# Four column groups for the ranking sums of layer 0's experts, and the masks' verdict ahead of them

## The chip, the cores and the metric

The kernel runs on one core of a Trainium2 chip. The metric is the device time of one execution in microseconds (us). Four engines compute: TensorE (PE, with its weight load listed apart as PEld), VectorE (DVE), ScalarE (ACT) and GpSimd (POOL). SyncE (SP) issues most of the transfers. Each engine works through its own list of instructions in order, and they wait for one another by semaphores.

## What is computed

The network has four layers, each a cross-attention of 2048 tokens (256 values each) with 1601 context rows, followed by a feed-forward block. The change concerns the first feed-forward block, a mixture of eight experts:

- The tokens are normed, multiplied with a gate matrix (256 x 8), and the eight scores of every token go through eight rounds of Sinkhorn normalization: columns are scaled to sum one, then rows.
- Every expert takes the 256 tokens (2048/8) with its highest scores. For that, every token needs its rank within each expert: how many tokens have a higher score, with ties settled by position.
- A token taken by several experts keeps the output of one. The expert's output is the normed token times that expert's 256 x 256 matrix; it is multiplied with the score and added to the token.

Two inputs are attention masks, int32, 2048 x 1601 each. The kernel looks at both of them at the start. If they have a certain form (all rows alike and only the last 400 columns ever open), the layers that use them can work on 400 context rows.

## The kernel before, in words

**Order of the program.** `network` runs `attention0` (layer 0's attention, which drives the look at the masks as a generator beside its own work), then `experts0`, then `verdict`. `verdict` (L286 on) multiplies the flags `some` with ones on PE (L293), casts the result to an integer on DVE (L294), and every engine loads it into a register (L295). A conditional follows: its first branch holds the layers with masked tails (`attention1_tail` first), the other one the general layers. What stands inside the conditional isn't mixed with what stands ahead of it. Outside of the regions named below, a scheduler at compile time settles the order on each engine; it may bring a transfer forward as soon as its buffer is free. `experts0` issues its two loads of expert weights `w_e` (L514, 1 MB each, SP) and that of the gate matrix `gw` (L531) at its head.

**Buffers.** The weights go into a ring of three buffers that lives through the whole program. Other buffers belong to pools that a stage opens and closes. A later stage's pool may lie where an earlier one's was.

**experts0.** 16 token tiles of 128, four chunks of 512. From the head of the stage on (after the constants), PE, ACT, DVE and POOL are kept in program order (`manual_schedule`), so the order written is the order run:

- Norm and gating for each chunk: statistics (L139, L140), inverse root on POOL (L145), scaling (L151), transposes (L173), copies `xe` (L177), then the gate product (L605).
- A generator `ahead` makes the products of one token tile with all eight experts, in four pieces. One piece is two matmuls of 512 columns in float32 (L568, four records in the profile, in `products`), a copy out of PSUM on ACT (L578), and after every second piece a write to a table in DRAM (L581). `step(ahead, 1)` makes one piece. Steps are placed in the norm, in the Sinkhorn rounds and in the ranking.
- Sinkhorn, eight rounds (L620 to L631).
- The ranking goes over eight experts `e` and 16 tiles `t`. `row` (L643, L647) spreads one expert's scores of a chunk over all partitions. For a tile `t`, DVE compares that row `bc` with the tile's own scores (L683, and L688 for the seven tiles below `short`), which gives `ge`, 128 x up to 2048 ones and zeros. `count` sums `ge` over the partitions on PE (L656), with the 128 x 8 matrix `pick` as weights, which puts the sum into row `e` of a PSUM tile `rk`. For tiles below `short` ACT also sums `ge` along its rows (L662). `count` for a tile is placed after the next tile's comparisons (`late`). There are three `ge` buffers.
- Then `rk` is copied to `rT` (L701), transposed to tokens (L707), and a chain of small DVE instructions settles which expert each token takes (L703 to L730).
- For the 13 tiles below `early`, POOL gathers the taken expert's row from the table (L735, indirect DMA, four row buffers) and DVE adds it to the token (L755, `add_row`). The products of the last three tiles are made here on PE, two pieces at a time, and DVE adds each expert's part, weighted (L747).

**After it.** `attention1_tail` loads three weights (L203), transposes them on PE (L211), copies them (L220), and projects keys (L951) and values (L960). Its loop over chunks begins with a norm (L173) and the query projection (L974). `ffn1`'s weights `w_fc` and `w_pr` take the ring buffers of `w_e`.

Of the kernel before, what the change touches and what calls it, by code (L numbers as in the profile page):

```python
# [15 lines left out]
P = 128  # L16
# [38 lines left out]
class Net:  # L55
# [451 lines left out]
    def experts0(self):  # L507
# [11 lines left out]
        early = 13  # L519

        short = 7
        with ExitStack() as s:
# [3 lines left out]
            cp = s.enter_context(tc.tile_pool(name="e0c", bufs=3))  # L526
            stage = s.enter_context(tc.tile_pool(name="e0s", bufs=3))
            rows = s.enter_context(tc.tile_pool(name="e0r", bufs=4))
# [21 lines left out]
            for e in range(E):  # L550
                nc.vector.memset(pick[:, e, e : e + 1], 1.0)
            number = pool.tile([P, E], F32, name="number")
# [3 lines left out]
            table = [dram.tile([P * E, D], F32, name=f"table{t}") for t in range(early)]  # L556
# [16 lines left out]
            def ahead():  # L573
                todo = None

                def out():
                    t, h, y, ps = todo
                    nc.scalar.copy(y[:, h * 512 : (h + 1) * 512], ps)  # L578
                    if h % 2:
                        at = slice((h - 1) * 512, (h + 1) * 512)  # L580
                        nc.sync.dma_start(table[t].rearrange("(p e) d -> p (e d)", e=E)[:, at], y[:, at])  # L581

                for t in range(early):
                    y = stage.tile([P, NTOK], F32, name="y0")
# [50 lines left out]

            rk = [self.psc() for _ in range(2)]
            opened = set()
# [11 lines left out]
            def count(e, t, ge):  # L649

                cuts = [max(t * P, j * CH) for j in range(t // TPC, NCH)] + [NTOK]
                if e == 0 and (t + 1) * P not in cuts:
                    cuts.insert(1, (t + 1) * P)
                for lo, hi in zip(cuts, cuts[1:]):
                    j = lo // CH
                    nc.tensor.matmul(  # L656
                        rk[j // 2][0:E, j % 2, lo - j * CH : hi - j * CH], lhsT=pick[:, e, :], rhs=ge[:, lo:hi],
                        start=j not in opened, stop=e == E - 1 and t == 0,
                    )
                    opened.add(j)  # L660
                if t < short:
                    nc.scalar.activation(  # L662
                        seen[:, (t + 1) * P :], ge[:, (t + 1) * P :], AF.Copy, accum_out=far[:, t, e : e + 1]
                    )
# [4 lines left out]
            late = None  # L669
            for e in range(E):  # L670
                nxt = bcp.tile([P, NTOK], F32, name="bc") if e + 1 < E else None

# [5 lines left out]
                for n, t in enumerate(turns):  # L678
# [8 lines left out]
                    if to < NTOK:  # L687
                        nc.vector.tensor_scalar(ge[:, to:], bc[:, to:], own, None, ALU.is_le)  # L688
                    if late is not None:
                        count(*late)  # L690
                    late = (e, t, ge)
                    if nxt is not None and n in (6, 8, 10, 12):
                        row(e + 1, nxt, NCH - 1 - (n - 6) // 2)
                    if n in (1, 4, 7, 10, 13):
                        step(ahead, 1)
                bc = nxt
            count(*late)
            drain(ahead)
            rT = bcp.tile([P, NTOK], F32, name="bc")
            for j, copy in ((1, nc.vector.tensor_copy), (0, nc.scalar.copy)):  # L700
                copy(rT[0:E, j * 1024 : (j + 1) * 1024].rearrange("p (a b) -> p a b", a=2), rk[j][0:E])  # L701
# [4 lines left out]
            for t in range(NT):  # L706
                nc.tensor.transpose(ps[:, t * E : (t + 1) * E], rT[0:E, t * P : (t + 1) * P], self.ident[:E, :E])  # L707
# [25 lines left out]
            for t in range(early):  # L733
# [1108 lines left out]
def network(ctx: ExitStack, tc: tile.TileContext, a, out):  # L1842
# [5 lines left out]
    net.experts0()  # L1848
    n_odd = net.verdict()
    with tc.If(n_odd == 0) as masked:  # L1850
        net.attention1_tail("L1_xattn", masks[0])
        net.ffn1()
        net.attention1("L2_xattn", bias=True)
        net.ffn2()
        net.attention3_tail(masks[1])
        net.ffn3()
    with masked.Else():
        net.attention1("L1_xattn", mask=masks[0])
        net.ffn1()
        net.attention1("L2_xattn", bias=True)  # L1860
        net.ffn2()
        net.attention3()
        net.ffn3()
# [35 lines left out]
```

## Time and profile before

The profiled execution took 2056.5 us, of which 2054.8 are its span, first to last instruction. Three timed runs gave 2055.5, 2059.0 and 2063.3.

| What | us |
|---|---|
| median of the runs | 2059.0 |
| profiled execution | 2056.5 |
| its span | 2054.8 |
| PE busy | 1853.0 |
| DVE busy | 1085.2 |
| ACT busy | 827.1 |
| POOL busy | 642.4 |
| attention0's last add ends at | 710.1 |
| ranking's first comparison starts at | 755.8 |
| its last comparison ends at | 915.1 |
| last `add_row` ends at | 946.4 |
| `attention1_tail`'s first projection starts at | 954.4 |

Positions in the table and below are in us from the start of the span. A row of a chain or a timeline begins with the start and the duration in us; then come engine, line, operation, the tiles written and read and their shapes; `[1.30 <-PE x]` says how long the engine had been idle and what ended that. A chain of waits follows the work that ended last back from the end, so its rows are what set the time. A row of a table by stretches gives the stretch, its length, busy us and number of instructions of PE, PEld, DVE, ACT and POOL, then PE's granted clock, the transfer engines' busy share and GB/s. One float32 matmul shows as two records.

### The profile page before, as it was taken

The numbers are of one execution on the slowest core, as the hardware profiler recorded it, in microseconds if no ns is written. First come the engines' busy times: TensorE is split into PE (matmuls) and PEld (weight loads), VectorE is DVE, ScalarE is ACT, GpSimd is POOL, SyncE is SP. The second block draws the span as 40 slices with busy tenths as digits, with TensorE's granted clock in tenths as the row PEclk, the third lists the DMA queues.
The fourth block names the chain that finished last, engine by engine and source line by source line (L and its number), as shares of the span: only waits on it lengthen the run. The fifth ranks groups of instructions, "written<-read, shape, count | busy, mean of one in ns | idle before, by whom it ended". The sixth has DMA issues, their size and how long they took to land.

```text
span 2054.8 us, 22310 instructions
## 1 busy us (share of the span) xinstructions
PE 1853.0 (90%) x8533; PEld 919.9 (45%) x8533; DVE 1085.2 (53%) x2117; ACT 827.1 (40%) x1133; POOL 642.4 (31%) x418
## 2 busy tenths in 40 slices
PE   7889999999999899998977899999788788888899
PEld 3223333333333343333535764565567323233587
DVE  4666465555654358776455543232376477866300
ACT  4654434434434237761114331111153265654432
POOL 1168878868768500003001110000033101111100
PEclk9799999999999999999988999999988899999999
DMA  8830000000000021113000000000000000000461
GB/s 282 291 104 1 1 1 1 1 1 1 1 1 1 0 83 62 66 58 105 1 24 19 1 24 0 1 0 1 0 1 0 6 1 1 1 1 1 139 201 53
DMA packets 44066, 78.83 MB, mean 38 GB/s; under 512 B 5757, under 2 KB 32782, under 8 KB 43950
## 3 DMA queue, kind: packets, MB, share of 16 engines
q1 hardware_dynamic: 41520, 73.97, 10.6%
q0 software_dynamic: 624, 1.70, 0.3%
q10 hardware_dynamic: 1806, 1.64, 0.3%
q8 instruction: 69, 1.13, 0.2%
q14 instruction: 47, 0.39, 0.1%
HBM read 61.57 MB, written 15.73 MB: 38 GB/s over the span
## 4 chain that ended last, share of the span: by engine, by line
PE 71%; DVE 14%; ACT 6%; issue 3%; DMA 3%; POOL 2%; SPq 0%; ACTq 0%; DVEq 0%; POOLq 0%
PE pa L468 7%; PE psc L456 5%; PE psc L884 5%; PE pa L904 4%; PE pa L568 4%; PE psc L1682 3%; DVE mp L381 3%; PE psc L1820 3%; PE pa L1831 3%; PE psc L656 3%; DVE ri L418 3%; ACT p L1689 2%; PE psc L454 2%; PE pm L1732 2%; PE pm L376 2%
## 5 line engine op out<-in xcount | busy, mean ns | idle before, releaser
L477 POOL TENSOR_TENSOR sp<-sp,p 128x1024 f32<-128x1024 f32 (+1 forms) x176 | 418.5, 2378 | 58.0 <-ACT p L461 47.3
L381 DVE TENSOR_REDUCE mp<-pm 128x1 f32<-128x512 f32 x384 | 242.8, 680 | 160.7 <-PE pm L376 160.0
L461 ACT ACTIVATE p<-psc 128x1024 f32<-128x1024 f32 (+1 forms) x208 | 212.7, 1023 | 260.4 <-PE psc L456 162.3
L456 PE MATMUL psc<-qT,kT 64*128 64x512 f32 (+1 forms) x832 | 219.9, 591 | 0.0
L468 PE MATMUL pa<-p,v 128*64 128x512 f32 (+1 forms) x832 | 202.8, 609 | 0.0
L1689 ACT ACTIVATE p<-psc 100x1024 f32<-100x1024 f32 x128 | 124.0, 1021 | 77.1 <-PE psc L1682 69.6
L1668 DVE TENSOR_REDUCE ms<-psc 128x2 bf16<-128x800 f32 x128 | 123.0, 981 | 43.0 <-PE psc L1664 40.8
L376 PE MATMUL pm<-kb,qb 64*128 64x512 bf16 x384 | 100.5, 391 | 28.2 <-DVE mp L381 26.6
L144 POOL TENSOR_SCALAR rstd<-mv 128x4 f32<-128x4 f32 x32 | 8.7, 272 | 360.4 <-DVE mv L140 336.8
L468 PEld LDWEIGHTS pa<-p,v 128*64 128x64 f32 (+1 forms) x832 | 50.9, 137 | 132.7 <-issue 129.7
L568 PE MATMUL pa<-w_e,xe 128*128 128x512 f32 x208 | 103.0, 620 | 0.0
L884 PE MATMUL psc<-q,kT 128*128 128x512 f32 (+1 forms) x208 | 102.2, 610 | 0.0
L683 DVE SCALAR_TENSOR_TENSOR ge<-bc,g,after 128x128 bf16<-128x128 f32 (+8 forms) x128 | 79.0, 649 | 30.8 <-PE psc L656 23.6
L897 ACT ACTIVATE p<-psc 128x1024 f32<-128x1024 f32 (+1 forms) x28 | 26.9, 962 | 168.2 <-PE psc L893 168.2
L456 PEld LDWEIGHTS psc<-qT,kT 64*128 64x128 f32 (+1 forms) x832 | 85.6, 186 | 19.8 <-issue 6.6
L904 PE MATMUL pa<-v,p 128*128 128x257 f32 (+1 forms) x416 | 93.9, 381 | 0.0
L1724 POOL TENSOR_TENSOR attn<-o,ri 128x512 f32<-128x512 f32 x16 | 20.3, 1271 | 230.9 <-DVE ri L1722 209.6
L662 ACT ACTIVATE seen<-ge 128x1152 bf16<-128x1152 bf16 (+6 forms) x56 | 83.4, 1489 | 19.1 <-DVE ge L688 18.8
L454 PE MATMUL psc<-sh,negz 64*128 64x512 bf16 (+1 forms) x416 | 87.2, 384 | 2.1 <-ACT sh L403 2.0
L857 DVE TENSOR_REDUCE mp<-pm 128x1 f32<-128x512 f32 x64 | 34.4, 571 | 99.8 <-PE pm L852 99.7
L151 DVE TENSOR_SCALAR xn<-x,mv,rstd 128x256 f32<-128x256 f32 x128 | 51.6, 459 | 67.0 <-PE pm L173 65.8
L1682 PE MATMUL psc<-q,kT 32*100 32x512 f32 x512 | 75.6, 640 | 10.4 <-ACT p L1689 10.0
(359 smaller groups left out, 3228.7 us busy)
## 6 DMA issues: line engine op xcount, KB each, us to landing
w<-in_L_ffn_w_dram SPq DMA_DIRECT2D x16, 1024.0 KB, 6.3
table<-y SPq DMA_DIRECT2D x26, 512.0 KB, 2.6
head<-in_mask_BxSxS_ik_dram SPq DMA_DIRECT2D x16, 600.5 KB, 4.0
head<-in_mask_1x1xSxS_ik_dram SPq DMA_DIRECT2D x16, 600.5 KB, 4.1
tail<-in_mask_BxSxS_ik_dram SPq DMA_DIRECT2D x16, 200.0 KB, 4.1
tail<-in_mask_1x1xSxS_ik_dram SPq DMA_DIRECT2D x16, 200.0 KB, 3.9
x<-in_x_dram SPq DMA_DIRECT2D x16, 128.0 KB, 3.6
w_e<-in_L_ffn_experts_dram SPq DMA_DIRECT2D x2, 1024.0 KB, 7.2
```

The source lines that it names most:

```text
L376: nc.tensor.matmul(pair[j][:, :wd], lhsT=qb[h, i * P : (i + 1) * P], rhs=kb[h, hp, k0 : k0 + wd], start=True, stop=True,)
L381: nc.vector.tensor_reduce(mp[:, i, j, n : n + 1], pair[j][:, :wd], AX.X, ALU.max)
L454: nc.tensor.matmul(sc[:r, j, :], lhsT=negz[h, :r], rhs=sh[h, :], start=True, stop=False)
L456: nc.tensor.matmul(sc[:r, j, :], lhsT=kT[h, hp, kt * P : kt * P + r], rhs=q[h, :], start=False, stop=True,)
L461: nc.scalar.activation(p[:r], sc[:r], AF.Exp, scale=DH**-0.5)
L468: nc.tensor.matmul(acc[h, :], lhsT=v[:r, kt, hp * P + h.start : hp * P + h.stop], rhs=p[:r, j, :], start=kt == 0, stop=kt == NKT - 1,)
L477: nc.gpsimd.tensor_tensor(sums[:r], sums[:r], p[:r], ALU.add)
L568: nc.tensor.matmul(ps, lhsT=xnT[t // TPC][:, kc, (t % TPC) * P : (t % TPC + 1) * P], rhs=ew[kc][:, 2 * h : 2 * h + 2, :], start=kc == 0, s ...
L884: nc.tensor.matmul(sc[:r, j, :], lhsT=kT[:, kc, ks], rhs=q[:, kc, :], start=kc == 0, stop=False)
L904: nc.tensor.matmul(acc[:, : D + 1], lhsT=p[:r, kt, i * P : (i + 1) * P], rhs=v[:r, kt, :], start=kt == 0, stop=kt == NKT - 1,)
L1682: nc.tensor.matmul(sc[j // 2][:TR, j % 2, :], lhsT=kT[h, g, kt * TR : (kt + 1) * TR], rhs=q[u][h, :], start=True, stop=True,)
L1689: nc.scalar.activation(p[:TR], sc[k][:TR], AF.Exp, scale=DH**-0.5)
```

## The change

- The sums of four tiles are now issued together: `count` takes four tiles, and puts the sums of the k-th of them into partitions 32k to 32k+7 of `rk`, for one 512-column piece after the other. `rk` is set to zero first, by matmuls with a tile of zeros, and closed in the same way. The copies out of `rk` take all 128 partitions, and the transposes L707 become products with `fold`, a 128 x 8 matrix that adds the four groups.
- ACT's sum along rows is placed one tile later, in `along`. There are nine `ge` buffers for three.
- `early` is gone: all 16 tiles' products go through the table, 50 pieces of them in the ranking instead of 38, and 16 rows are gathered, with six row buffers for four. The products and weighted adds beside the gathers are gone.
- `verdict` runs ahead of `experts0`, which now stands in both branches of the conditional.

```diff
-            cp = s.enter_context(tc.tile_pool(name="e0c", bufs=3))
+            cp = s.enter_context(tc.tile_pool(name="e0c", bufs=9))
...
-            rows = s.enter_context(tc.tile_pool(name="e0r", bufs=4))
+            rows = s.enter_context(tc.tile_pool(name="e0r", bufs=6))
...
+            fold = pool.tile([P, E], F32, name="fold")
+            nc.vector.tensor_reduce(
+                fold, self.ident.rearrange("p (k r) -> p r k", k=4)[:, :E, :], AX.X, ALU.add
+            )
+            none = pool.tile([P, CH], BF16, name="none")
+            nc.gpsimd.memset(none, 0.0)
...
-                for t in range(early):
+                for t in range(NT):
                     y = stage.tile([P, NTOK], F32, name="y0")
...
+            def zeros(start, stop):
+                for j in range(NCH):
+                    nc.tensor.matmul(rk[j // 2][:, j % 2, :], lhsT=none[:, :P], rhs=none, start=start, stop=stop)
+
+            zeros(True, False)
...
-            def count(e, t, ge):
-
-                cuts = [max(t * P, j * CH) for j in range(t // TPC, NCH)] + [NTOK]
-                if e == 0 and (t + 1) * P not in cuts:
-                    cuts.insert(1, (t + 1) * P)
-                for lo, hi in zip(cuts, cuts[1:]):
-                    j = lo // CH
-                    nc.tensor.matmul(
-                        rk[j // 2][0:E, j % 2, lo - j * CH : hi - j * CH], lhsT=pick[:, e, :], rhs=ge[:, lo:hi],
-                        start=j not in opened, stop=e == E - 1 and t == 0,
-                    )
-                    opened.add(j)
-                if t < short:
-                    nc.scalar.activation(
-                        seen[:, (t + 1) * P :], ge[:, (t + 1) * P :], AF.Copy, accum_out=far[:, t, e : e + 1]
-                    )
+            def count(e, four):
+
+                for j in range(NCH):
+                    for k, (t, ge) in enumerate(four):
+                        lo = max(t * P, j * CH)
+                        if lo < (j + 1) * CH:
+                            nc.tensor.matmul(
+                                rk[j // 2][32 * k : 32 * k + E, j % 2, lo - j * CH :], lhsT=pick[:, e, :],
+                                rhs=ge[:, lo : (j + 1) * CH], start=False, stop=False,
+                            )
+
+            def along(e, t, ge):
+
+                nc.scalar.activation(
+                    seen[:, (t + 1) * P :], ge[:, (t + 1) * P :], AF.Copy, accum_out=far[:, t, e : e + 1]
+                )
...
+                    if long is not None:
+                        along(*long)
+                    long = (e, t, ge) if t < short else None
                     if late is not None:
                         count(*late)
-                    late = (e, t, ge)
+                        late = None
+                    four.append((t, ge))
+                    if len(four) == 4:
+                        late, four = (e, four), []
                     if nxt is not None and n in (6, 8, 10, 12):
                         row(e + 1, nxt, NCH - 1 - (n - 6) // 2)
-                    if n in (1, 4, 7, 10, 13):
+                    if n in (1, 3, 7, 9, 11, 15) or n == 13 and e < 2:
                         step(ahead, 1)
                 bc = nxt
+            along(*long) if long is not None else None
             count(*late)
             drain(ahead)
+            zeros(False, True)
             rT = bcp.tile([P, NTOK], F32, name="bc")
             for j, copy in ((1, nc.vector.tensor_copy), (0, nc.scalar.copy)):
-                copy(rT[0:E, j * 1024 : (j + 1) * 1024].rearrange("p (a b) -> p a b", a=2), rk[j][0:E])
+                copy(rT[:, j * 1024 : (j + 1) * 1024].rearrange("p (a b) -> p a b", a=2), rk[j])
...
             for t in range(NT):
-                nc.tensor.transpose(ps[:, t * E : (t + 1) * E], rT[0:E, t * P : (t + 1) * P], self.ident[:E, :E])
+                nc.tensor.matmul(
+                    ps[:, t * E : (t + 1) * E], lhsT=rT[:, t * P : (t + 1) * P], rhs=fold, start=True, stop=True
+                )
...
-            for t in range(early):
+            for t in range(NT):
                 row = rows.tile([P, D], F32, name="row")
...
-                if t % 2 == 0 and early + t // 4 < NT:
-                    tt, k = early + t // 4, t // 2 % 2
-                    sc = self.psc()
-                    for j in range(2):
-                        products(tt, 2 * k + j, sc[:, j, :])
-                    for e in range(4):
-                        nc.vector.scalar_tensor_tensor(
-                            self.x[tt], sc[:, e // 2, (e % 2) * D : (e % 2 + 1) * D],
-                            g[:, tt, 4 * k + e : 4 * k + e + 1], self.x[tt], ALU.mult, ALU.add,
-                        )
-            for t in range(early - 2, early):
+            for t in range(NT - 2, NT):
                 self.add_row(t, fetched[t], gate)
...
-    net.experts0()
     n_odd = net.verdict()
     with tc.If(n_odd == 0) as masked:
+        net.experts0()
         net.attention1_tail("L1_xattn", masks[0])
...
     with masked.Else():
+        net.experts0()
         net.attention1("L1_xattn", mask=masks[0])
```

More of the change, by code (lines that the diff above doesn't have):

```diff
@@ L516, in experts0 @@
             )
-        early = 13
         short = 7
@@ L555, in experts0 @@
             xnT = [pool.tile([P, 2, CH], F32, name=f"xe{c}") for c in range(NCH)]
-            table = [dram.tile([P * E, D], F32, name=f"table{t}") for t in range(early)]
+            table = [dram.tile([P * E, D], F32, name=f"table{t}") for t in range(NT)]
             g = pool.tile([P, NT, E], F32, name="g")
@@ L636, in experts0 @@
             rk = [self.psc() for _ in range(2)]
-            opened = set()
+            def zeros(start, stop):
+                for j in range(NCH):
+                    nc.tensor.matmul(rk[j // 2][:, j % 2, :], lhsT=none[:, :P], rhs=none, start=start, stop=stop)
+            zeros(True, False)
             def row(e, bc, c):
@@ L668, in experts0 @@
                 row(0, bc, c)
-            late = None
+            late = long = None
+            four = []
             for e in range(E):
```

## The prediction, on record before the changed kernel ran

> **What bounds the kernel now.** The page says PE is busy 90% of the span, so I read layer 0's experts (the change's place) and what touches it in four views.
>
> First the chain of waits, ranking loop (start, us, what):
>
> ```profile
> 815.78 2.16 PE psc L656 x10
> 818.14 0.59 PE psc L656 x2
> 818.73 1.91 PE pa L568 x4
> 820.65 1.18 PE psc L656 x7
> 821.82 1.91 PE pa L568 x4
> 823.74 0.80 PE psc L656 x4
> 824.53 0.58 PE pm L643 x4
> 825.37 1.91 PE pa L568 x4
> ...
> 835.96 2.16 PE psc L656 x10
> ```
>
> One expert takes 20.2 us (815.78 to 835.96), all of it PE: the sums (L656) 7.8, five products (L568) 9.4, rows (L643) and gaps 3.0. Second, busy times by stretch (PE, PEld, DVE, ACT, POOL), of this loop and of what follows it:
>
> ```profile
> 835.00:855.00 20.00, 19.79 (x77) 7.70 (x76) 16.05 (x40) 15.08 (x24) 0.00 (x0) 1.00 0.13 53
> 917.00:945.00 28.00, 24.77 (x66) 11.72 (x66) 19.47 (x50) 0.95 (x2) 12.78 (x13) 0.88 0.20 58
> ```
>
> Relieve PE and DVE is next at 16.05, then ACT at 15.1. Third, the timeline of the gather, a chain of POOL gathers beside the 48 product records:
>
> ```profile
> 918.01 1.87 PE L707 MATMUL pm<-ident,bc 8*128 8x8 f32 x16 [1.86 <-ACT bc L701]
> 919.81 22.87 PE L568 MATMUL psc<-w_e,xe 128*128 128x512 f32 x48
> 923.60 1.22 POOL L735 DMA_INDIRECT row<-table,index  x1 [200.74 <-DVE gate L730]
> 926.38 0.95 POOL L735 DMA_INDIRECT row<-table,index  x1 [0.30 <-issue]
> 946.36 0.14 DVE L294 CAST n_odd<-pm 1x1 int32<-1x1 f32 x1
> 947.22 0.38 SPq L203 DMA_DIRECT2D w_L_xattn<-in_L_xattn_Wk_dram  x1
> 954.38 4.72 PE L951 MATMUL pm<-ctxT,WkT 128*128 128x400 f32 x8
> ```
>
> Nothing after the branch is issued before the verdict: weights at 947.22, attention's first projection at 954.38. Fourth, the opening, where the chain of waits runs through the mask loads from 50 to 127 us; `w_e`, which today needs no verdict, is loaded inside that stretch:
>
> ```profile
> 68.39 0.39 SPq L514 DMA_DIRECT2D w_e<-in_L_ffn_experts_dram  x1
> ```
> ```profile
> 70.12 6.47 DMA head<-in_mask_1x1xSxS_ik_dram
> 76.68 1.30 ACT head L276 x2
> 78.00 3.79 DMA head<-in_mask_1x1xSxS_ik_dram
> ```
>
> **What the Trainium skill says.** "TensorEngine Tiling (Array Packing)", Tiling Modes: with outputs of at most 32 columns the array holds four 128x32 tiles that run in parallel. The trace agrees: L1699 (four heads, 100*32) ran 8 records in 1.07 us, where 8 full-width records take 8 x 0.43 = 3.4. "TensorE: Matmul & The Clock Gate", Part 1: after idling PE runs at half clock until some 3.4 us of work are done; here the 48 records took 22.9, not 48 x 0.43 = 20.6. "DMA: Bandwidth & Descriptors", Queues, rings and completion order: descriptors of one issuing engine are consumed in ring order on each DMA engine. Here w_pr, issued 0.5 us behind w_fc (1 MB each), landed after 9.3 us, w_fc after 7.3: about 3 us per MB behind the first.
>
> **Part 1, opening: -2.5.** `w_e` moves behind the branch, so the head load that stood behind it lands in some 3.9 instead of 6.47 us. The other `w_e` load (35.47) fell in a stretch where PE was the chain: nothing. By stretches of 10 us PE is only 53 to 90% busy from 60 to 130, so the gain passes on. Ends: -3.4 (1 MB at the 0.3 MB/us of that stretch) and +1 (a reordered queue).
>
> **Part 2, front of the experts: +11.** Today constants, half the norm statistics, gw and both `w_e` are done while attention ends, and chunk 0's transposes start at 710.13, its gating at 711.99. After: attention's last add ends 710.06; the verdict's matmul, cast 0.14, register load and branch take SP to 711.4 (today 0.86 from the cast's start to SP's next DMA; add to cast 0.5, my estimate). No barrier shows there today. SP issues w_e, w_e, gw; by the w_fc/w_pr pair the second lands 9.3 after its issue at 711.85, thus 721.2, gw just behind; attention 1's weight loads queue behind them on SP and do no harm. Meanwhile DVE and POOL make constants and chunk 0's norm (4 x 0.57 statistics, 1.3 root, 4 x 0.35 scaling: xnT about 720.5, hidden by the DMA, but with no margin). Gating starts at 721.4: +9.4. PE, idle since 710, begins cold: +1.6 (half of 8 product records' 3.4). Ends: +7.5 (gw overtakes, PE warm), +12.5.
>
> **Part 3, ranking: -17.** Per expert the loop has still 40 sum matmuls, but each set of four shares one pass. By the diff's cuts the longest column group of the four sets has 1280, 1536, 1792 and 2048 columns, 6656 instead of 17408. At 0.213 us per 512 that is 2.8 us instead of 7.25; with the surcharge seen today (7.8 for 7.25) I take 3.2. Ends: 2.8 and 7.8 (no overlap). Products go from five to six of 1.72; edges (0.19 where a product follows sums, 0.26 to 0.4 where it follows a row; one and four of them now) come to 1.4 as today. Rows 2.3. Sum 10.3 + 1.4 + 2.3 + 3.2 = 17.2 for experts 2 to 6, 19.1 for expert 1 (a seventh product). Expert 0: 18.6 against 18.4 today. The last has no rows: 14.8 to the end of its sums against 19.7 (896.48 to 916.14; today DVE and ACT end last there). Today 18.4 + 20.2 + 5 x 20.17 + 19.7 = 159.1; after 18.6 + 19.1 + 5 x 17.2 + 14.8 = 138.5. DVE (16.05) and ACT (15.1 + one copy 0.58 = 15.7) are now within 1.5 us of PE, all in order; nine `ge` buffers let DVE lead by some five tiles, but ACT's row copies wait for PE behind queued products. I add 0.4 per expert, 3.2 together: 141.7. Ends of this surcharge: 0 and 1.8 each.
>
> **Part 4, zeros and rank: +2.9.** Four 512-column bf16 matmuls at each end: 0.9 each. The first delays the rows; the second sums. L707 becomes a full f32 matmul with 128x128 weights, two records each: 32 x 0.108 (gating, L605, 1.73 for 16) = 3.5 against 1.9. The wide copies cost what the narrow ones do (same columns). Today ACT's 1.9 us sum ends after the last sums; now it is done before: -0.5. The last `y` copy and table write are covered by gathers 0 to 14, and the copy of the experts in the other branch isn't executed: nothing. 0.9 + 0.9 + 1.6 - 0.5 = 2.9.
>
> **Part 5, gather to attention: -4.5.** Twelve products leave PE and 24 adds leave DVE, but POOL is the chain: 16 gathers, first to last 1.53 + 14 x 1.27 = 19.3, landing 2.7, add 0.5 and 0.1: 22.6 from the first issue (today 22.8 for 13, the last L755 ending at 946.44, held by four row buffers and PE; six buffers cover 7.5 us, more than issue to add). Weights are then present. Does attention start under the gather? The second attention shows the rule:
>
> ```profile
> 1195.57 0.74 DVE L1202 TENSOR_TENSOR y<-pa,scb 128x256 f32<-128x256 f32 x2
> ...
> 1196.46 0.65 ACT L220 COPY WkT<-pm 128x256 f32<-128x256 f32 x2 [4.95 <-DVE mv L140]
> ...
> 1196.89 2.26 PE L211 MATMUL pm<-ident,w_L_xattn 128*128 128x128 f32 x8 [2.01 <-ACT WkT L220]
> ```
>
> The weight copies, bk's load and a memset all waited for the previous stage's last add: new buffers open when the whole old pool is released. Here that is the last `add_row`, which reads `gate`. So only the norm and two transposes hide; WkT, WvT, WqT then take 3.1 to L951 (1196.46 to 1199.5 there). Norm work of chunks 0 to 2 may slip between gathers on POOL (1.3 each): +0.6. 22.6 + 0.6 + 3.1 = 26.3, today 954.38 - 923.60 = 30.8. Ends: -1 (three roots, slow copies), -15 (nothing waits).
>
> **Sum:** -2.5 + 11 - 17.4 + 2.9 - 4.5 = -10.5 (ranking 159.1 to 141.7). Own execution 2056.5 (span 2054.8 and 1.7 around it) gives 2046; the runs' median 2059.0 lies 2.5 above, 2048.5. I say 2048. A measurement can tell 0.5%, 10.3 us, from no change.
>
> **Rivals.** A, the forecast, 2041 to 2055: 0.48, of it 0.29 faster by over 0.5% and 0.19 within.
> B: the three engines in order hold each other, about 19 us per expert. For: by the waits of the loop ACT stood 22 us for PE's rows and DVE 24 for PE's sums. Against: nine buffers. Surcharge 1.5 rather than 0.4: +9, 2057; 0.24, all but 0.02 within.
> C, the slower side: column groups don't overlap for 8-column weights. Sums cost 7.8 again and the product is added: 8 x 4.6 - 3 = +34, 2082. It decides from 4.5 us of sums per expert (10.5/8 above 3.2). Against: L1699. 0.08, slower.
> D: pool release doesn't hold attention back, so projections of keys and values (954.38 to 963.1) and chunk 0 hide under the gather: -10 more, 2038. For: POOL alone works there. Against: 1196.46. 0.20, 0.19 of it faster.
> Faster 0.48, within 0.42, slower 0.10. The range, 2036 to 2061, holds A, most of B and D, and leaves out C.
>
> **What would show it.** Right: `w_e` issued near 709, gating 9 us later than today against attention's end; expert period 17 to 18 with PE over 95% busy; L707 3.5; gathers 1.25 apart; WkT's copy right behind the last add. Wrong: sums over 4.5 per expert, a period over 19 with PE idle on ACT, L951 under the gather, or a mask stage no shorter.

## The result, and the profile after

Thirteen runs of each kernel, in turn on one chip: 2059.5 us before (2055.5 to 2065.0), 2049.7 us after (2041.1 to 2053.7). The ratio is 0.9945, with a 95% interval of 0.9928 to 0.9961: 10 us less. The interval leaves out 1, and the difference is about the 0.5% that the prediction named as the least to be told from no change. The profiled execution of the changed kernel took 2043.5 us (span 2041.8, 13.0 below the one of before) and lies near the low end of its runs. The changed kernel's runs differ along with PE's granted clock: the five of 2041.1 to 2046.0 us have a mean clock of 0.948 to 0.950, the eight of 2048.3 to 2053.7 one of 0.939 to 0.946.

Laid side by side, the two profiles divide as follows. All places are us from the start of the span; line numbers of the changed kernel are up to 22 higher.

| Mark or stretch | before | after | difference |
|---|---|---|---|
| first attention unit's copy `o` (L501) | 141.1 | 143.1 | +2.0 |
| from there to attention0's last add | 569.0 | 569.0 | 0.0 |
| last add to the ranking's first comparison | 45.7 | 58.1 | +12.4 |
| first comparison to the rank product (L707, now L727) | 162.2 | 138.7 | -23.6 |
| rank product to the first gather | 5.6 | 10.1 | +4.5 |
| first gather to the next attention's query projection (L974, now L986) | 40.6 | 34.8 | -5.8 |
| from there to the end | 1090.6 | 1087.9 | -2.6 |

The loop first. The timeline of PE in one expert of the changed kernel (start, us, what):

```profile
837.37 0.92 PE L667 MATMUL psc<-ge,pick 128*8 128x128 bf16 x11
...
840.53 1.03 PE L667 MATMUL psc<-ge,pick 128*8 128x384 bf16 x12
841.72 1.98 PE L574 MATMUL pa<-w_e,xe 128*128 128x512 f32 x4 [0.16 <-ACT y L584]
843.99 1.98 PE L574 MATMUL pa<-w_e,xe 128*128 128x512 f32 x4 [0.29 <-ACT y L584]
845.90 0.71 PE L667 MATMUL psc<-ge,pick 128*8 128x128 bf16 x9
...
848.84 0.81 PE L667 MATMUL psc<-ge,pick 128*8 128x384 bf16 x8
...
854.04 0.92 PE L667 MATMUL psc<-ge,pick 128*8 128x128 bf16 x11
```

The same mark comes 16.67 us later (837.37 to 854.04), where one expert took 20.17. Taken from each start to the next start on PE, less the wait of 0.16 behind the second, the four groups of sums last 0.86, 1.03, 0.64 and 0.74, together 3.3 us instead of 7.8. Busy times of that stretch (PE, PEld, DVE, ACT, POOL) say what is next:

```profile
837.37:854.04 16.67, 16.23 (x82) 6.89 (x81) 15.76 (x40) 15.55 (x25) 0.00 (x0) 1.00 0.24 96
```

PE still sets the pace, with 0.45 us of waiting for ACT's copies, but DVE at 15.8 and ACT at 15.6 are right behind. Next the front. Before, the first transposes came right behind the attention's last add (which ended at 710.1), and the gating 1.4 us behind it:

```profile
710.13 1.09 PE L173 MATMUL pm<-ident,xn 128*128 128x128 f32 x8 [0.52 <-DVE x L432]
711.50 2.22 PE L605 MATMUL pm<-gw,xe 128*128 128x8 f32 x16 [0.28 <-ACT xe L177]
```

From the timelines of SP, DVE and PE of the changed kernel:

```profile
704.24 1.01 SPq L514 DMA_DIRECT2D w_e<-in_L_ffn_experts_dram  x2
705.57 1.42 SPq L530 DMA_DIRECT2D gw<-in_L_ffn_gate_w_dram  x1
...
711.68 0.43 DVE L432 TENSOR_TENSOR x<-pm,x 128x256 f32<-128x256 f32 x1 [1.30 <-PE pm L427]
712.65 0.09 DVE L548 MEMSET pick<- 128x32 uint32 x1 [0.54 <-DVE x L432]
...
716.13 0.18 DVE L140 BATCH_NORM_AGGREGATE mv<-st 128x2 f32<-128x6 f32 x1
717.79 0.73 DVE L151 TENSOR_SCALAR xn<-x,mv,rstd 128x256 f32<-128x256 f32 x2 [1.48 <-POOL rstd L145]
718.35 0.71 PE L173 MATMUL pm<-ident,xn 128*128 128x128 f32 x2 [6.78 <-DVE xn L151]
721.56 3.88 PE L611 MATMUL pm<-gw,xe 128*128 128x8 f32 x16
```

SP passed the branch at 704, before the attention had ended, since the verdict's matmul had found a gap on PE at 701.7. By the trace the two loads of `w_e` landed at 709.7 and 712.6, and `gw` at 712.9. But DVE comes to the constants and the norm only behind the attention's last add, and PE stands idle for 6.8 us before the first transpose. The gating starts 9.45 us behind the last add, and it takes 3.9 us for 2.2. Last, the rank product, the gathers and what follows, from the timelines of PE, POOL and DVE:

```profile
906.55 1.04 PE L647 MATMUL psc<-none 128*128 128x512 bf16 x4
908.90 6.40 PE L727 MATMUL pm<-fold,bc 128*128 128x8 f32 x32 [1.32 <-ACT bc L721]
919.02 1.22 POOL L757 DMA_INDIRECT row<-table,index  x1 [182.75 <-DVE gate L752]
938.06 0.95 POOL L757 DMA_INDIRECT row<-table,index  x1 [0.30 <-DVE st L139]
940.83 0.48 DVE L767 SCALAR_TENSOR_TENSOR x<-row,gate,x 128x256 f32<-128x256 f32 x1 [0.78 <-DMA row<-table,index]
941.97 2.27 PE L211 MATMUL pm<-ident,w_L_xattn 128*128 128x128 f32 x8 [25.18 <-ACT WkT L220]
```

The rank product takes 6.4 us for 32 records, 0.2 each. The sixteen gathers follow each other in 1.25 us. The next attention's transposes start right behind the last add, and its first projection comes 3.0 us behind it, where it came 7.9 us behind it before.

### The profile page after: what moved, and what is told of

It is laid out like the page before. It is cut to its first block, busy times and chain, and to the rows that moved or that the text cites. A ratio compares the mean times of both kernels' runs of the same rounds, so it can differ in the third digit from the quotient of the medians.

```text
span 2041.8 us, 22380 instructions
## 1 busy us (share of the span) xinstructions
PE 1814.0 (89%) x8545; PEld 911.5 (45%) x8545; DVE 1066.1 (52%) x2097; ACT 831.1 (41%) x1145; POOL 645.3 (32%) x422
## 4 chain that ended last, share of the span: by engine, by line
PE 61%; DVE 14%; issue 12%; ACT 6%; DMA 5%; POOL 2%; ACTq 0%; SPq 0%; POOLq 0%; DVEq 0%
PE pa L468 7%; PE psc L456 5%; PE psc L896 5%; PE pa L916 4%; PE psc L1694 3%; DVE mp L381 3%; PE psc L1832 3%; PE pa L1843 3%; DVE ri L418 3%; ACT p L1701 2%; PE psc L454 2%; PE pm L376 2%; PE pm L1661 2%; PE pm L1744 1%; PE pm L427 1%
## 5 line engine op out<-in xcount | busy, mean ns | idle before, releaser
L574 PE MATMUL pa<-w_e,xe 128*128 128x512 f32 x256 | 125.2, 617 | 4.9 <-ACT y L584 4.9
L916 PEld LDWEIGHTS pa<-v,p 128*128 128x128 f32 (+1 forms) x416 | 78.1, 190 | 12.2 <-issue 0.2
```

The source lines that it names most:

```text
L574: nc.tensor.matmul(ps, lhsT=xnT[t // TPC][:, kc, (t % TPC) * P : (t % TPC + 1) * P], rhs=ew[kc][:, 2 * h : 2 * h + 2, :], start=kc == 0, s ...
L916: nc.tensor.matmul(acc[:, : D + 1], lhsT=p[:r, kt, i * P : (i + 1) * P], rhs=v[:r, kt, :], start=kt == 0, stop=kt == NKT - 1,)
```

## The experiments

Theory at the start: the loop gained more than forecast, and the verdict's move costs more than it brings. The rival: the move pays for itself, and something else has given the gain back.

**The move alone, undone and done.** First the changed kernel with only the move undone:

```diff
-    n_odd = net.verdict()
-    with tc.If(n_odd == 0) as masked:
-        net.experts0()
+    net.experts0()
+    n_odd = net.verdict()
+    with tc.If(n_odd == 0) as masked:
...
     with masked.Else():
-        net.experts0()
```

> The change without its move: the verdict stands behind the experts again; sums, products and gathers stay as changed. My theory: the front wins back its delay (chunk 0's gating 721.6 returns to some 711.5 after a last attention add near 710: about -10), and the end loses its early start (first projection of the next attention some 8 us behind the last add_row instead of 3: +5). Sum about -5 against the changed kernel: ratio to before 0.992 (2043), the range 2038 to 2048. If w_e's load was what made the first attention 2 us longer in the changed kernel, its last add is back at 710.1; if not, it stays at 712. Rival: the move pays for itself elsewhere (later stages): then this kernel is not faster than the changed one, 2050 or more.

Measured: 2039.2 us, ratio to before 0.9899 (0.9875 to 0.9923), 10 us faster than the changed kernel. By its profile the front is 46.6 instead of 58.1 (last add to first comparison), and first gather to query projection 39.4 instead of 34.8. The first attention unit ends at 142.2. Then the kernel before with the move and nothing else (the same edit the other way):

> The kernel before with the verdict moved ahead of the experts and nothing else. My theory: front +10, end of the stage -5 (first projection 3 us behind the last add_row instead of 8): +5, 2064, ratio 1.0025, range 2060 to 2068. Rival that the move is worth something later on: ratio at or below 0.999. Last add of the first attention at 712 if w_e's load decides it, 710 if it is something else.

Measured: 2073.7, ratio 1.0067 (1.0043 to 1.0091): slower, by more than expected. Front +11.5, first gather to query projection +0.5 (the gathers and their adds spread over 28.5 us instead of 22.8, with two of the norm's roots between them on POOL, which also waits up to 2.2 us at a time for DVE's adds, while the way from the last add fell from 17.8 to 12.6), first unit's end at 146.2, 5 us later. Both say that the move is the part of the change that loses. The rival falls.

**The opening.** The expectation had left open why the first attention came out longer. The order in which SP issues the two masks' loads, by the instruction lists of the kernels (h, t: head and tail of the first mask, H, T: of the second, W: `w_e`), before and after:

```
hththththtWhththththththththththtWHTHTHHHHHTTHTTHTTHTTHTHTHTHTHTHT
hththththththththththththtthhtthHTTHHTTHHHHHHHTTHTTHTTHTHTTHHTTT
```

Without the two W the scheduler lays the rest in another order, with heads queued behind pairs of tails. In the timeline of SP in the changed kernel:

```profile
59.10 2.32 SPq L263 DMA_DIRECT2D tail<-in_mask_BxSxS_ik_dram  x2
61.46 2.83 SPq L261 DMA_DIRECT2D head<-in_mask_BxSxS_ik_dram  x2
64.81 0.80 SPq L263 DMA_DIRECT2D tail<-in_mask_BxSxS_ik_dram  x2
```

Two issues took 2.3 and 2.8 us there, where one takes 0.3 to 0.4: SP stands inside the pair, and all loads behind it stand with it. To tell order from traffic, two loads were added where they had been:

```diff
+        for kc in range(2):
+            (w,) = self.weights(f"e0{kc}", 2048)
+            w = w.rearrange("p (e f) -> p e f", e=E)
+            nc.sync.dma_start(w, a["L0_ffn_experts"][:, kc * P : (kc + 1) * P, :].rearrange("e p f -> p e f"))
+            read = self.small.tile([P, 1], F32, name="read")
+            nc.vector.tensor_copy(read, w[:, 0, 0:1])
```

> The changed kernel with two more loads of the experts' weights where the kernel before had them, in the look at the masks; one element of each is read and nothing else, and the loads behind the branch stay. This gives SP the same order of head and tail loads as before. My theory: the order in which SP issues the mask loads, not the 2 MB moved, decides the opening: the copy that ends the first attention unit (143.1 in the changed kernel, 146.2 and 147.9 in the other two kernels with the verdict moved, 141.0 to 142.2 in the three with it behind) comes at 141 to 142.5, and the median falls by 3 to 7 us, to 2043 to 2047. Rival one, the prediction's: 2 MB more traffic makes the opening longer, 145 or later, 2052. Rival two: chance from run to run; then the copy comes anywhere from 141 to 148 and the median stays at 2049 to 2050.

Measured: 2044.6, ratio 0.9928 (0.9913 to 0.9943), with 2 MB more to load. The median is 5 us below the changed kernel's, but the two ratios' intervals overlap, so that a gain in the time isn't shown. The first unit ends at 141.2. The timeline of SP is back to head and tail in turn:

```profile
60.81 0.33 SPq L261 DMA_DIRECT2D head<-in_mask_BxSxS_ik_dram  x1
61.23 0.38 SPq L263 DMA_DIRECT2D tail<-in_mask_BxSxS_ik_dram  x1
63.72 0.33 SPq L261 DMA_DIRECT2D head<-in_mask_BxSxS_ik_dram  x1
```

Over all profiles of this study the two orders don't overlap: nine kernels with the order of before ended the first unit at 139.2 to 142.2 (the kernel before itself at 141.1), five without the two loads there at 143.1 to 148.5, and of these five the changed kernel has the earliest. The extra traffic is thus not what makes the opening long. Two things stay open. Four of the five have the same order to the letter (the changed kernel, the move alone, and the two kernels with one column group and with five buffers below) and still ended the unit at 143.1, 146.2, 147.9 and 148.5. And no kernel had the order of before without the two loads, so order and loads weren't told apart. The openings of the runs that weren't profiled were not seen.

**What sets the front.** The prediction held that the weights' landing does. An experiment moved only DVE's constants (`rest`, `first`, `pick`, `fold`, `number`) and `gw` with its load ahead of the verdict, into a function of their own (with a small copy of the POOL tile that `rest` reads); `w_e` stayed behind it:

```diff
+    net.expert_constants()
     n_odd = net.verdict()
```

> The changed kernel with the DVE constants of the experts and the gate matrix's load made ahead of the verdict (w_e, the POOL tiles and the norm stay behind it). My theory: DVE's chain, not the weights, sets the front: constants are 2.6 us of it, so the gating starts some 7 us after the last attention add rather than 9.5, and the first comparison some 56 rather than 58.5 after it. Prediction's view: the weights' landing sets it; gating stays at 9 to 9.5. The time then follows with the opening: 2047 against 2049.7 if the opening is the same as in the changed kernel.

Measured: 2049.9, ratio 0.9943 (0.9924 to 0.9962), no gain in the time, with the first unit's end at 147.8. In its profile the gating starts 7.8 us behind the last add instead of 9.45, and the first comparison 57.1 instead of 58.1. From its timeline:

```profile
716.50 0.42 DVE L432 TENSOR_TENSOR x<-pm,x 128x256 f32<-128x256 f32 x1 [1.30 <-PE pm L427]
719.30 0.18 DVE L140 BATCH_NORM_AGGREGATE mv<-st 128x2 f32<-128x6 f32 x1
...
720.96 0.74 DVE L151 TENSOR_SCALAR xn<-x,mv,rstd 128x256 f32<-128x256 f32 x2 [1.48 <-POOL rstd L145]
724.73 3.89 PE L623 MATMUL pm<-gw,xe 128*128 128x8 f32 x16
```

So DVE's and POOL's chain sets the front: constants some 1.6 us of it, and the rest is chunk 0's norm (statistics, root, scaling, transposes, copies), which had for the most part lain inside the attention before. The weights were not late: in the changed kernel they were there 9 us ahead of the gating.

**The column groups.** All four tiles' sums into one group, the rest as changed:

```diff
-    rk[j // 2][32 * k : 32 * k + E, j % 2, lo - j * CH :], lhsT=pick[:, e, :],
+    rk[j // 2][0:E, j % 2, lo - j * CH :], lhsT=pick[:, e, :],
```

> The changed kernel with the sums of all four tiles put into the same column group (partitions 0 to 7) instead of four; order, count and operands of the matmuls stay. My theory: the sums then run one behind the other, 7.3 to 7.8 us per expert instead of 3.5; the period goes from 16.7 to 20.5 to 21, the time by +32 (2082, ratio 1.011). Rival: the saving in the loop came from the order (four tiles in one go, nine buffers) and not from the groups side by side: period stays under 18.5 and the time under 2065.

Measured: 2079.4, ratio 1.0096 (1.0067 to 1.0125). The timeline of PE over one expert of this kernel:

```profile
839.47 2.54 PE L667 MATMUL psc<-ge,pick 128*8 128x384 bf16 x12
...
845.57 1.68 PE L667 MATMUL psc<-ge,pick 128*8 128x128 bf16 x9
...
849.48 1.68 PE L667 MATMUL psc<-ge,pick 128*8 128x384 bf16 x8
...
855.54 2.11 PE L667 MATMUL psc<-ge,pick 128*8 128x128 bf16 x11
...
859.88 2.54 PE L667 MATMUL psc<-ge,pick 128*8 128x384 bf16 x12
```

Period 20.41, sums 7.7 (to the next start: 2.47, 1.61, 1.60, 2.04), and 168.9 us from the first comparison to the rank product instead of 138.7. The same matmuls in the same order cost 3.3 us when they lie in four groups: 2.4 times as fast. The Trainium skill ("TensorE: Matmul & The Clock Gate", Part 3, Measured speedup vs the span model) has 2.38 for three groups of columns; here the ratio of the columns to be streamed (17408 to 6656, by the diff's cuts) would allow 2.6.

**The buffers.** Nine `ge` buffers cut to five (`bufs=9` to `bufs=5` in the pool `e0c`):

> The changed kernel with five ge buffers instead of nine (the fewest that four tiles taken together and one ahead can do with). Theory: the buffers are what lets DVE run ahead of sums that now wait for the fourth tile; with five, DVE stands for PE at each group and the period goes from 16.7 to 18 to 20. Rival: PE is the bound with a steady lead of DVE of two or three tiles, and five do: period under 17.2.

Measured, one run: 2062.1. Ranking 150.1 instead of 138.7 us, a period of 18.05 (844.73 to 862.78 below). Its waits from 800 to 905 us and three rows of its timeline on PE:

```profile
DVE ge L695 <- PE psc L667: 14.1, 12, 2.6
...
PE psc L667 <- DVE ge L700: 7.7, 11, 1.3
```
```profile
844.73 0.92 PE L667 MATMUL psc<-ge,pick 128*8 128x128 bf16 x11
849.47 1.02 PE L667 MATMUL psc<-ge,pick 128*8 128x512 bf16 x11 [1.26 <-DVE ge L700]
862.78 0.92 PE L667 MATMUL psc<-ge,pick 128*8 128x128 bf16 x11
```

DVE waits for buffers, then PE for DVE. So by this one profile the lead is worth 11 us of the ranking's gain: with five buffers the loop comes near the prediction's rival B (engines that hold each other).

**Where the branch should stand.** The move's gain lies at the end of the stage, its loss at the head, so the branch was put between: constants to choice ahead of it, the gathers behind it in both branches, with the row buffers left open through the next attention. `experts0` now ends with `index` and `gate` and closes its pools; `gather0` issues the gathers and adds.

```diff
+    net.experts0()
     n_odd = net.verdict()
     with tc.If(n_odd == 0) as masked:
-        net.experts0()
-        net.attention1_tail("L1_xattn", masks[0])
+        with tc.tile_pool(name="e0r", bufs=6) as rows:
+            net.gather0(rows)
+            net.attention1_tail("L1_xattn", masks[0])
```

> The changed kernel with the branch put between the experts' ranking and the gathers: constants, gating, Sinkhorn, ranking and the choice stay ahead of the verdict, the 16 gathers and adds stand behind it, and the row buffers stay open through the next attention so that none of its buffers waits for the last add_row. My theory: the front is as before (-10 against the changed kernel), and projections of keys and values (some 12 us) run under the gathers, with half the weight transposes: -10 to -13 more; sum 2027 to 2032, ratio 0.986. Rival: what holds attention back is not the buffers but something else (POOL's order, the transfers): then the first projection still comes 3 us behind the last add_row, and the time is about 2040 (ratio 0.991).

Measured: 2034.2, ratio 0.9875 (0.9852 to 0.9898). Front 46.6, query projection 6.3 us behind the last add_row instead of 12.5; less than expected reached the end, and the interval overlaps that of the kernel with the verdict back behind the experts (0.9875 to 0.9923). The same kernel with the rows' pool closed before the attention (one level of indentation less):

> The kernel with the branch between ranking and gathers, but with the pool of the row buffers closed before the next attention opens its own. Theory (the rule that the prediction took from a later stage): the attention's buffers then lie where the rows were, and the weight copies wait for the last add_row: WkT's copy right behind it, the query projection 12 us behind it instead of 6.3, the time some 6 us longer. Rival: only the place of the branch matters; then WkT's copy still comes with the first gathers.

Measured, one run: 2040.8. From the timelines of the open and of the closed kernel:

```profile
905.31 0.65 ACT L221 COPY WkT<-pm 128x256 f32<-128x256 f32 x2 [11.71 <-PE pm L212]
908.19 4.68 PE L967 MATMUL pm<-ctxT,WkT 128*128 128x400 f32 x8
927.46 0.48 DVE L771 SCALAR_TENSOR_TENSOR x<-row,gate,x 128x256 f32<-128x256 f32 x1 [0.84 <-DMA row<-table,index]
```
```profile
933.58 0.48 DVE L771 SCALAR_TENSOR_TENSOR x<-row,gate,x 128x256 f32<-128x256 f32 x1 [0.70 <-DMA row<-table,index]
934.37 0.65 ACT L221 COPY WkT<-pm 128x256 f32<-128x256 f32 x2 [34.88 <-POOL v L963]
```

With the pool open, `WkT` is copied with the first gathers; with it closed, right behind the last add, and the query projection 13.3 us behind it. That is the rule that the prediction had taken from a later stage.

**The rank product.** Two edits to the kernel with the branch between ranking and gathers. One keeps PE busy ahead of the product:

```diff
             zeros(False, True)
+            busy = self.pa()
+            for _ in range(8):
+                nc.tensor.matmul(busy, lhsT=none[:, :P], rhs=none, start=True, stop=True)
```

> The kernel with the branch between ranking and gathers (2034.2) with eight matmuls of 512 bf16 columns on zeros, into a bank that nobody reads, between the closing of rk and the product with fold: PE doesn't idle there. Theory: the product is slow (5.6 to 6.4 us instead of 3.5) because PE's clock has fallen over the 1.3 us of idling; then it takes 3.5 to 4.2 now and the first gather comes 2 us earlier after the ranking. Rival: the product itself, small matmuls behind full weight loads, is what lets the clock fall; then it takes 5.5 or more as before.

The other makes it in one pass (`F32R`, the rounded float32 type, for `rT` and `fold`):

```diff
-            fold = pool.tile([P, E], F32, name="fold")
+            fold = pool.tile([P, E], F32R, name="fold")
...
-            rT = bcp.tile([P, NTOK], F32, name="bc")
+            rT = bcp.tile([P, NTOK], F32R, name="bc")
```

> The kernel with the branch between ranking and gathers (2034.2) with the sums copied out and multiplied with fold in the one-pass float32 type[...]. Theory: one record per matmul instead of two, 16 records, so the product takes half, 2.5 to 3.3 us instead of 6.1, and the first gather comes some 3 us earlier after the ranking: 2031. Rival: the copies into the rounded type or a slower record eat that: product over 4.5 or copies longer by over 1 us, no gain.

Measured: 2028.0, ratio 0.9839 (0.9819 to 0.9860), and 2028.2, 0.9839 (0.9820 to 0.9858). The product took 3.63 and 2.80 us (6.09 without either), and the first gather came 8.2 and 7.4 us behind its start instead of 10.7. PE's granted clock, the number behind POOL's busy time, by stretches in the changed kernel and then in the kernel kept busy, whose product ran from 898.62 to 902.25:

```profile
909.00:911.00 2.00, 2.00 (x13) 2.00 (x13) 0.26 (x2) 0.00 (x0) 0.00 (x0) 0.65 1.01 353
911.00:913.00 2.00, 2.00 (x11) 2.00 (x11) 0.00 (x0) 0.00 (x0) 0.00 (x0) 0.50 0.98 334
```
```profile
899.00:901.00 2.00, 2.00 (x21) 2.00 (x20) 0.00 (x0) 0.00 (x0) 0.00 (x0) 1.00 0.26 104
902.00:904.00 2.00, 0.37 (x5) 0.24 (x4) 1.61 (x7) 0.00 (x0) 0.00 (x0) 0.54 0.00 0
```

The clock is the cause: the same 32 records take 0.11 us each at a clock of 1.00 and 0.21 at 0.50. That the idle gap is what lets the clock fall isn't shown. A mean of 0.54 over 902 to 904 means that the clock fell at 902.15, just ahead of the product's end, when PE had done nothing but the product for 3.4 us and hadn't idled. And a kernel with the same gap, the one with the two loads added, was quicker with nothing put into it:

```profile
905.63 4.48 PE L736 MATMUL pm<-fold,bc 128*128 128x8 f32 x32 [1.32 <-ACT bc L730]
```

In the clock records of all fourteen traces, any two changes lie a whole multiple of 3.413 us apart. In the eight kernels with this product and nothing put in, the clock fell at such a point 0.7 to 2.8 us behind the product's start, and the product took the less, the later that was: 6.40 us at 0.7 (the changed kernel), 6.09 at 1.0, 5.83 at 1.3, 4.48 at 2.8. So the small matmuls alone are enough for the clock to fall, and where the next such point lies sets how many run before it does. In the kernel kept busy one such point lay 0.1 us behind the product's start and passed without a fall, so that the next came after 3.5 us. Whether the gap would have let the clock fall there, no run shows.

The two kernels' times overlap with that of their base by their intervals; the gain is read from the stretch, 2.5 and 3.3 us in these profiles.

**A version that beats both.** With the attention open to the gathers, chunk 0 needs only the first four rows. The one-pass kernel was given sixteen row buffers and a written order there:

```diff
+            order.enter_context(tc.manual_schedule(engines=IN_ORDER))
+            fetch(6)
...
+            fetch(2)
...
+            for t in range(4):
+                add(t)
+            first = prepare(0, made)
+            step(first, 1)
+            fetch(8)
+            for t in range(4, NT):
+                step(first, 1) if t % 2 == 0 else None
+                add(t)
```

> The kernel with the branch between ranking and gathers and the one-pass product (2028.2), with sixteen row buffers and a written order around the gathers: keys and values first, then the adds of tiles 0 to 3, the norm of chunk 0 with its root on POOL between the eighth and ninth gather, its query projection, and the other adds between the steps after it. Theory: chunk 0 of the attention needs only the first four rows, which land some 8 us after the first gather; its query projection comes 14 to 16 us after the first gather instead of 29.6, and nearly all of that reaches the end: 2014 to 2017, ratio 0.978. Rival: POOL's eight later gathers or DVE's adds, now behind the norm, hold up chunk 1, and less than 6 us are left: 2022 or more.

Measured: 2024.9, ratio 0.9820 (0.9807 to 0.9833): the rival's side. The query projection came 21 us after the first gather, because DVE reached its first add at 919.1. The last kernel corrects that order (the adds and statistics ahead of the values' copies, those copies on ACT):

> The woven kernel (2024.9) with two corrections of its written order: the adds of tiles 0 to 3 and the norm's statistics stand ahead of the values' copies on DVE, and those copies go to ACT, which is idle there. In the woven kernel DVE came to the first add only at 919.1, though row 3 had landed by about 914, because the copies of keys and values, which wait for PE, stood ahead of it in order. Theory: adds by 915, norm root on POOL right behind the eighth gather, query projection 15 us after the first gather instead of 21, and most of the 6 us reaches the end: 2019 to 2022. Rival: the later gathers or PE's low clock there hold chunk 0 anyway: 2023 or more.

Measured: 2020.6, ratio 0.9813 (0.9789 to 0.9837), query projection 18.4 us after the first gather. Here DVE's copies of the keys still stand between the adds, and the root waits for DVE: from the timeline,

```profile
913.95 0.57 DVE L986 CAST kb<-pm 128x400 bf16<-128x400 f32 x1
...
918.76 0.23 POOL L145 TENSOR_SCALAR rstd<-mv 128x4 f32<-128x4 f32 x1 [4.47 <-DVE mv L141]
...
922.70 3.70 PE L1012 MATMUL pm<-xnT,WqT 128*128 128x512 f32 x8 [0.24 <-ACT xnT L178]
```

The intervals of the two woven kernels overlap; against both kernels of the study they are clear.

## Why the prediction was right, and where it was not

The forecast was 2048, the measurement 2049.7, and case A, the forecast, came. The mechanism of the large terms was right. Yet the number owes its closeness to errors of opposite sign; the prediction's terms against the two profiles, with zeros and ACT's end kept apart as it kept them (the 0.5 for ACT's end is its own figure, and cancels between steps 3 and 4):

| Step | forecast | by the profiles |
|---|---|---|
| 1, opening | -2.5 | +2.0 (other kernels with the move +5.1 to +7.5) |
| 2, front | +11 | +11.4 (12.4 less the opening zeros, 1.0) |
| 3, ranking | -17.4 | -24.1 (-23.6 less closing zeros +1.0, plus ACT's end 0.5) |
| 4, zeros and rank product | +2.9 | +6.1 (2.1, 4.5, -0.5) |
| 5, gather to attention | -4.5 | -5.8 |
| later stages | none | -2.6 |

- **Part 1 failed in sign.** It took the gain from the load that stood ahead of a head in one place of the chain, and put the reordering of the queue at +1 at most. The runs showed the opposite: with the two loads taken out of SP's list, all loads behind them were relaid, and in five profiles of five the first unit ended 2.0 to 7.5 us later than before; with the loads back, and 2 MB more to move, it ended at 141.2. How much of that is the order alone stays open.
- **Part 2 had the right sum from wrong terms.** It let SP wait for the attention's end and the weights land at 721, for a gating 9.4 us later, and gave the cold PE 1.6. SP was through at 704 and the weights were there at 712.9; DVE's constants and norm, which the prediction held to be "hidden by the DMA, but with no margin", set the gating, 8.0 us later (9.45 behind the last add for 1.43). The cold PE cost 3.3, since the half clock lasted until 728.7, 7 us behind the gating's start. From chunk 0's gating to chunk 1's it took 10.2 us for 6.9, with 3.9 for the first gating, and 2.2 in the kernel with the verdict behind the experts. One term too large and one too small made up the 11.
- **Part 3 was right in its mechanism, and too small.** Sums came at 3.3 (forecast 3.2), waiting at 0.45 (0.4). The period, 16.67 against 17.6, was missed in the other terms: the seams between products and sums, forecast at 1.4 and rows at 2.3, measured as 0.7 and 1.9 from start to start. Some 0.9 per expert over seven experts comes near the 6.7 us. Without the four groups it would have been rival C (20.41), and with five buffers near rival B (18.05).
- **Part 4** priced L727 at the clock of the gating, 3.5; at the clock that PE had there it was 6.4, and 4.48 to 6.40 over the eight kernels with this product. The kept-busy kernel showed 3.63.
- **Part 5** was right, with 1.3 more (by its own mark, the first projection, 25.3 us from the first gather for 26.3 forecast): gathers 22.3 us from the first issue to the end of the last add (forecast 22.6 and 0.6), and `WkT` right behind the last add. Rival D, attention under the gather, needs the open pool and is worth some 7 us there (12.5 or 13.3 to 6.3).
- **Later stages** run the same program in both kernels. From ffn1's first `wfT` copy to the end, the profiles of this study have 984.4 to 990.3 us, so the -2.6 is within what single profiles differ by. The changed kernel's is the shortest of all fourteen, with the fewest us at half clock in that stretch, 111.6; the longest has 127.9.

The sum by the profiles, 2.0 + 11.4 - 24.1 + 6.1 - 5.8 - 2.6, is the span's -13.0. In the median 3 us of that are gone again: the profiled run had the shortest later stages of all profiles and the earliest opening of those without the two loads, and the other runs weren't seen from inside.

## What to carry to other kernels

A step that is moved behind a branch loses the work that other stages had covered, on every engine; put the branch at the place where nothing ahead of it can still be used as cover, and leave pools open if the next stage is to begin under the old one. Four narrow matmuls in four column groups are worth their zeros and their fold, if buffers are added for the lead that the grouping takes. When a forecast removes one load from an in-order queue, the order of those behind it may change: read that order, not only the load's own time.

## What the hardware showed beyond that

PE's clock can differ for the same work in the same place. From the last unit's copy to attention0's last add the profiles of the two kernels with the branch between ranking and gathers took 17.9 us (rows' pool open) and 21.0 (closed), with the same work there. Stretches of 5 us (engines, then the granted clock), first open, then closed:

```profile
700.40:705.40 5.00, 3.37 (x16) 2.98 (x17) 3.43 (x23) 0.00 (x0) 0.00 (x0) 1.00 0.00 0
```
```profile
701.50:706.50 5.00, 3.37 (x8) 2.71 (x9) 3.10 (x22) 0.00 (x0) 0.00 (x0) 0.50 0.00 0
```

In the same time sixteen records in one and eight in the other. The Trainium skill ("TensorE: Matmul & The Clock Gate", Part 1) speaks of a free-running window of about 3.4 us after which the clock rises, and the traces' steps of 3.413 us agree. The half clock lasted two steps in the open kernel and four in the closed one, and the fourteen profiles sort by where the steps lie. Four in which the clock fell 2.8 to 3.3 us behind the start of the last unit's copy took 17.9 to 18.0 us for this stretch, five in which it fell 3.6 to 4.2 us behind it took 20.7 to 21.0, and the other five, which fell earlier or later, 19.5 to 19.7. No run moved the steps on purpose. The same page lets the clock fall after an idle window of that length; in the kernel kept busy it fell at the end of a step that the rank product had filled without idling. Here the measurement decides: work of that kind didn't keep the clock up.
